# A fused cross-attention and ternary feed-forward kernel: the attention loop regrouped into beats of two key blocks

## The chip, the core and the metric

The kernel runs on one NeuronCore of a Trainium2 chip, as one launch. The core has four compute engines that run side by side, each through its own instruction stream in order: TensorE (PE in the profile, with its weight loads listed apart as PEld), VectorE (DVE), ScalarE (ACT) and GpSimd (POOL). SyncE (SP) only issues transfers here. Matrix products land in PSUM, everything else lives in SBUF; DMA queues move data, and a DMA issued by POOL can add into its target on the way. The metric is device time in microseconds, lower is better; it is given as the median of several runs.

## The reference

Shapes: `x` is 2048 x 256 (the latents), `ctx` is 1601 x 256, four heads of 64, hidden width 1024. Cut to what matters:

```python
lat = layernorm_g_b(layernorm(x));  c = layernorm_g_b(ctx)
q = lat @ W_q;   k, v = split(concat([c, lat]) @ W_kv)      # 1601 + 2048 keys
q, k = rmsnorm(q) / 8, rmsnorm(k)                           # per head of 64
sim = q @ k.T;   sim[:, masked ctx keys] = -big
x = x + (softmax(sim) @ v) @ W_out + b_out                  # 2048 x 256
h = act_quant(layernorm(x)) @ weight_quant(w1).T            # ternary weights, 2048 x 1024
h = silu(depthwise_conv3(h) + conv_b)
x = x + act_quant(h) @ weight_quant(w2).T
```

The softmax needs, for each query and head, the maximum over all keys before the exponentials and the sum of the exponentials after them.

## The kernel before

**Tiling.** The keys are padded to 29 blocks of 128 (`NKB`): blocks 0 to 12 are the context (`NCB` = 13, masked), blocks 13 to 28 are the latents. The queries are cut into four groups of 512, the heads into two pairs, which gives eight *units* `(g, pr)`. A unit works on a tile of keys x (2 heads x 512 queries), 128 x 1024 in float32: scores have the keys on the partitions. The two heads of a pair lie on partition halves, so a score product (`raw_scores`, line 176) is two products that each use 64 rows of the PE array, and a value product (`attend`, line 514) is two products that each fill 64 columns. In the profile the forms are called `64*128` and `128*64`; one float32 product shows as two records, so a block of scores or of values is a group of x4.

**Two passes over the scores.** While unit u is being attended, the scores of unit u+1 are computed once for their maxima (`look_ahead`, line 184, tile `sa`): a context block is copied out of PSUM with its mask added and kept in SBUF (ACT, tile `sg`, 14 buffers in `ring`), a latent block is not kept; DVE reduces either to its maxima (`mxs`). When all 29 blocks are seen, `column_maxima`, `transpose_maxima`, `row_maxima` and `spread_shift` (lines 451 to 495) turn them into the negative maximum per query, as a pair of bfloat16 rows (`rows`) and as a full tile (`nb`). In unit u+1 itself a kept block needs only `sg + nb` (`subtract`, line 498, on DVE) and the exponential on ACT (tile `pt`, five buffers); a latent block is computed again on PE on top of the broadcast shift (`again`, line 502, tile `st`: two bfloat16 products and one float32 score product, shown as x6) and then exponentiated.

**Sums and values.** `attend` adds each `pt` into a sum: context blocks and the last two on POOL (`acc`), the other latent blocks by accumulating DMAs from POOL's queue into `acd` (in the last unit by DVE), and multiplies `pt` with the values into `ot` in PSUM. `finish_unit` (line 540) copies `ot` out on ACT, joins the two sums on POOL, and forms the reciprocal denominators in five further planned pieces: 16 products (`dn`), a reciprocal, eight diagonal matrices on ACT (`dg`), 16 products that spread them (`rd`), a multiply. After every second unit `finish_block` (line 593) runs four times: output projection `po`, residual, layer norm and activation quantization of 128 rows each, the result transposed (`tpq`). In the last unit `weight_tasks` (line 707) quantizes and transposes the feed-forward weights.

**Order.** The loop over steps (lines 745 to 788) takes one key block per step, latent and context blocks in turn, and emits in this order: the exponential two steps on, the look-ahead of one block (sometimes two), the subtraction three steps on or the repeated scores two steps on, then `attend`, then whatever `at(k, ...)` has planned for that step. `InOrder` (line 157) keeps this order on each engine, so all these instructions carry line 165 in the profile, and they are told apart by their tiles. PSUM has three two-bank buffers for scores (`big`, line 148, used by `sa`, `st` and `sh`), one single bank (`bank`) for small results, and one for `ot`. After the loop the feed-forward part runs in `slot(s)` (line 933), with the tail of the plan taken before each slot.

Of the kernel before, what the change touches and what calls it, by code (L numbers as in the profile page):

```python
# [17 lines left out]
P = 128  # L18
# [8 lines left out]
def kernel(  # L27
# [386 lines left out]
    def at(k, *calls):  # L414

        plan.setdefault(k, []).extend(calls)
# [30 lines left out]
    with att:  # L447
# [13 lines left out]
        def transpose_maxima(m4):  # L461
            tp = bank("tpm", [P, P])
            tensor.transpose(tp, m4.rearrange("p a b -> p (a b)"), ident)
            return tp

        def row_maxima(tp):

            nm = sm.tile([P, 32], F32, tag="nm", name="nm", bufs=2)
            vector.tensor_reduce(
                nm, tp.rearrange("p (a i) -> p i a", a=4), AX.X, ALU.max, negate=True  # L470
            )
            hi = sm.tile([P, 32], BF16, tag="hi", name="hi", bufs=2)
            vector.tensor_copy(hi, nm)
            val = sm.tile([P, 32], F32, tag="val", name="val", bufs=2)
# [23 lines left out]
        def subtract(u, j):  # L498

            vector.tensor_tensor(staged[u, j], staged[u, j], shifts[u][1], ALU.add)  # L500
# [13 lines left out]
        def attend(u, j, pt, ot, sums, i):  # L514


            g, pr = units[u]
            acc, acd = sums
            if j < NCB or i >= NKB - 2:
                if j == 0:  # L520
                    gpsimd.tensor_copy(acc, pt)
                else:
                    gpsimd.tensor_tensor(acc, acc, pt, ALU.add)
            elif u == len(units) - 1:
                if i == 0:
                    vector.tensor_copy(acd, pt)
                else:
                    vector.tensor_tensor(acd, acd, pt, ALU.add)
            elif i == 0:
                gpsimd.dma_start(acd, pt)  # L530
            else:
                gpsimd.dma_start(acd, pt, accum_op=ALU.add)
            for hh in range(2):
                h = 2 * pr + hh
                tensor.matmul(
                    ot[halves(hh), :], v_sb[:, j, h * DH : (h + 1) * DH], pt[:, hh, :],
                    start=(i == 0), stop=(i == NKB - 1),
                )

        def finish_unit(k, ot, sums, dst):  # L540

            scalar.copy(dst, ot)
            box = {}
            acc, acd = sums

            def join():
                gpsimd.tensor_tensor(acc, acc, acd, ALU.add)

            def denominators():

                box["dn"] = bank("dn", [P, NSUB, 2])
                for sub in range(NSUB):
                    for hh in range(2):
                        tensor.matmul(
                            box["dn"][:, sub, hh : hh + 1], acc[:, hh, ts(sub, P)], ones[:, 0:1],
                            start=True, stop=True,
                        )

            def inverses():
                box["r"] = sm.tile([P, NSUB, 2], F32, tag="r", name="r", bufs=2)  # L560
                vector.reciprocal(box["r"], box["dn"])

            def diagonals():
                box["dg"] = ptp.tile([P, NSUB, 2, P], F32, tag="pt", name="dg")
                for sub in range(NSUB):
                    for hh in range(2):
                        scalar.activation(
                            box["dg"][:, sub, hh, :], ident, AF.Copy,
                            scale=box["r"][:, sub, hh : hh + 1],
                        )  # L570

            def spread_inverses():
                box["rd"] = bank("rd", [P, NSUB, P])
                for sub in range(NSUB):
                    for hh in range(2):
                        tensor.matmul(
                            box["rd"][halves(hh), sub, :], ones[:, :DH], box["dg"][:, sub, hh, :],
                            start=True, stop=True,
                        )

            def divide():
                vector.tensor_tensor(
                    dst, dst, box["rd"].rearrange("p s q -> p (s q)"), ALU.mult
                )

            for n, call in (
                (1, join), (3, denominators), (4, inverses), (5, diagonals), (6, spread_inverses),
                (7, divide),
            ):
                at(k + n, call)  # L590


        def finish_block(k, qb, oT, sub):
# [47 lines left out]
            for n, call in (  # L641
                (-2, bias), (0, project_out), (1, residual), (2, inverse_deviation), (3, normalize),
                (5, quantize), (6, transpose), (7, spread),
            ):
                at(k + n, call)
# [3 lines left out]
        def quantize_weight(src, i):  # L649
            w_sb, box = [], {}  # L650

            def load():
                for k in range(2):
                    t = ring.tile([P, 2 * QW], F32, tag="sg", name="w_sb")
                    nc.sync.dma_start(t.rearrange("p (a d) -> p a d", d=src.shape[2]), src[:, k])
# [51 lines left out]
        def weight_tasks(k):  # L707
# [5 lines left out]
            for n, call in enumerate(calls):  # L713
                at(k + n, call)
# [5 lines left out]
        order = [NCB + i // 2 if i % 2 == 0 else i // 2 for i in range(2 * NCB)]  # L720
        order += list(range(2 * NCB, NKB))
        early = {i: [i // 2] if i % 2 == 0 else [NCB + i // 2] for i in range(2 * NCB - 1)}
        for n, i in enumerate((6, 12, 18, 24)):
# [271 lines left out]
```

## Time and profile before

| | value |
|---|---|
| median of three runs | 994.49 us (994.21, 994.49, 1006.95) |
| the profiled execution | 1002.59 us, its span 1000.8 us |
| prologue: norms, keys, values, queries, maxima of unit 0 | 0 to about 162 us |
| the eight units: starts of the eight `nb` copies | 162.4, 243.4, 327.8, 422.8, 510.0, 598.3, 681.7, 773.3 us |
| feed-forward part: first `ph` product | 854.7 us, to the end |
| busy over the span: PE, DVE, ACT, POOL | 86%, 80%, 55%, 56% |
| mean granted TensorE clock | 0.906 |

The differences of the `nb` starts are the lengths of units 0 to 6: 81.0, 84.4, 95.0, 87.3, 88.3, 83.4 and 91.6 us, 610.9 us together. Units 2, 4 and 6 also carry the four `finish_block`s of the query group before; they are the longest on average. In the profile a group line gives the line, engine, operation, output from inputs, shapes and count, then busy time and mean duration, then the idle time just before and what ended it. The tile view gives shortest, median and longest duration instead. The chain of waits is the sequence of work, each piece released by the one before, that leads to the last instruction.

### The profile page before, as it was taken

To read this page: it belongs to the slowest core of one execution; us is meant where nothing else is said; L and a number is where in the kernel's file an instruction comes from. 1 tells how busy PE (TensorE), PEld (TensorE's weight loads), DVE (VectorE), ACT (ScalarE), POOL (GpSimd) and SP (SyncE) were. 2 spreads that over 40 slices of the span, in tenths; PEclk is the share of its full clock that TensorE was granted. 3 is DMA by queue.
4 is the path that set the end of the run, shared out by engine and by line. 5 is a ranking of instruction groups with operands and counts; after the bars stand their busy time and mean duration, and the time that the engine had idled before them with its cause. 6 is when DMAs were issued, how large, how long until landed. Compare 5 with 4: busy or idle time off the path is not lost.

```text
span 1000.8 us, 10358 instructions
## 1 busy us (share of the span) xinstructions
PE 859.9 (86%) x3672; PEld 328.0 (33%) x3672; DVE 797.1 (80%) x914; ACT 546.5 (55%) x738; POOL 560.7 (56%) x447
## 2 busy tenths in 40 slices
PE   4788987998999999899989999998998977656564
PEld 3334442322322332233223323223322322434342
DVE  4566456996898689968877987987899897399996
ACT  2456444554555555365555556555553634888792
POOL 2432332655565466555665677556666654777672
PEclk9999998999999899899999999999999977555557
DMA  5000001543455343434543444544434100000000
GB/s 135 22 22 22 1 0 43 105 85 84 84 98 101 77 84 71 77 85 84 105 95 74 85 83 92 100 86 103 84 69 101 63 1 18 4 12 10 13 20 32
DMA packets 29776, 63.28 MB, mean 63 GB/s; under 512 B 7259, under 2 KB 16668, under 8 KB 29724
## 3 DMA queue, kind: packets, MB, share of 16 engines
q0 software_dynamic: 14112, 51.39, 26.2%
q1 hardware_dynamic: 12030, 10.44, 3.4%
q10 hardware_dynamic: 3582, 0.79, 0.4%
q8 instruction: 29, 0.48, 0.2%
q14 instruction: 23, 0.19, 0.1%
HBM read 9.13 MB, written 2.10 MB: 11 GB/s over the span
## 4 chain that ended last, share of the span: by engine, by line
PE 55%; DVE 32%; ACT 5%; issue 4%; DMA 2%; POOL 2%; ACTq 0%; POOLq 0%; DVEq 0%
PE sa L165 16%; PE ot L165 16%; PE st L165 10%; DVE mxs L165 5%; DVE sg L165 5%; PE kv L353 5%; PE sa L179 3%; DVE m L165 2%; DVE y L165 2%; DVE acd L165 2%; DVE t L165 2%; DVE h L165 2%; DVE hi L165 1%; DVE rows L165 1%; DVE qsc L165 1%
## 5 line engine op out<-in xcount | busy, mean ns | idle before, releaser
L165 POOL TENSOR_TENSOR acc<-acc,pt 128x1024 f32<-128x1024 f32 x112 | 282.9, 2526 | 35.3 <-ACT pt L165 34.9
L165 PE MATMUL ot<-pt,v_sb 128*64 128x512 f32 x928 | 252.7, 629 | 2.0 <-ACT pt L165 1.9
L165 DVE TENSOR_TENSOR sg<-sg,nb 128x1024 f32<-128x1024 f32 x104 | 215.7, 2080 | 13.9 <-ACT nb L165 13.9
L165 PE MATMUL sa<-q_un,kT 64*128 64x512 f32 x812 | 223.7, 639 | 2.8 <-DVE mxs L165 2.8
L165 POOL DMA_DIRECT2D acd<-pt x98 | 83.9, 856 | 211.8 <-ACT pt L165 164.0
L165 ACT ACTIVATE sg<-sa,maskc 128x1024 f32<-128x1024 f32 x91 | 101.2, 1112 | 177.2 <-PE sa L165 176.9
L165 ACT ACTIVATE pt<-st 128x1024 f32<-128x1024 f32 x128 | 130.9, 1023 | 76.5 <-PE st L165 76.3
L165 DVE TRANSPOSE_TENSOR_REDUCE mxs<-sa 128x32 f32<-128x1024 f32 x112 | 137.4, 1232 | 35.9 <-PE sa L165 34.9
L165 DVE TRANSPOSE_TENSOR_REDUCE mxs<-sg 128x32 f32<-128x1024 f32 x91 | 112.7, 1238 | 38.5 <-ACT sg L165 38.5
L165 PE MATMUL st<-q_un,kT 64*128 64x512 f32 x512 | 141.1, 630 | 0.0
L165 ACT ACTIVATE pt<-sg 128x1024 f32<-128x1024 f32 x104 | 109.3, 1051 | 41.2 <-DVE sg L165 41.1
L165 PEld LDWEIGHTS sa<-q_un,kT 64*128 64x128 f32 x812 | 63.9, 185 | 137.8 <-issue 90.1
L165 PEld LDWEIGHTS ot<-pt,v_sb 128*64 128x64 f32 x928 | 48.4, 138 | 182.9 <-issue 173.7
L165 PEld LDWEIGHTS st<-q_un,kT 64*128 64x128 f32 x512 | 53.0, 201 | 34.6 <-issue 30.8
L353 PE MATMUL kv<-wkv_sb,feat 128*128 128x512 f32 (+1 forms) x116 | 55.8, 624 | 0.0
L165 PE MATMUL st<-rows,ones 64*128 64x512 bf16 x256 | 52.0, 400 | 1.5 <-DVE mxs L165 1.5
L329 DVE TENSOR_TENSOR nn<-raw,ss 128x512 f32<-128x512 f32 (+1 forms) x23 | 15.7, 681 | 47.0 <-POOL ss L101 47.0
L165 POOL TENSOR_TENSOR pre<-pre,side 128x512 f32<-128x512 f32 x32 | 41.8, 1306 | 14.6 <-DVE pre L165 13.3
L165 ACT ACTIVATE side<-h,cw_sb 128x256 f32<-128x256 f32 x96 | 44.4, 494 | 0.0
L165 PE MATMUL py<-w2T,hq 128*128 128x256 bf16 x128 | 30.4, 418 | 14.6 <-DVE hq L165 14.6
L165 ACT ACTIVATE pre<-h,cb_sb,cw_sb 128x256 f32<-128x256 f32 x64 | 37.4, 584 | 9.8 <-DVE h L165 9.7
L165 ACT ACTIVATE t<-pre 128x512 f32<-128x512 f32 x32 | 36.5, 1141 | 9.4 <-POOL pre L165 9.4
(131 smaller groups left out, 1002.2 us busy)
## 6 DMA issues: line engine op xcount, KB each, us to landing
acd<-pt POOLq DMA_DIRECT2D x98, 512.0 KB, 4.5
tok<-in_x_dram SPq DMA_DIRECT2D x4, 512.0 KB, 3.6
q_un<-in_x_dram SPq DMA_DIRECT2D x4, 512.0 KB, 3.6
w_sb<-in_L_ffn_w_dram SPq DMA_DIRECT2D x4, 512.0 KB, 3.3
out_dram<-res SPq DMA_DIRECT2D x16, 128.0 KB, 1.8
tok<-in_ctx_dram SPq DMA_DIRECT2D x3, 512.0 KB, 4.1
wkv_sb<-in_L_xattn_W_kv_dram ACTq DMA_DIRECT2D x1, 512.0 KB, 8.9
wo_sb<-in_L_xattn_W_out_dram SPq DMA_DIRECT2D x1, 256.0 KB, 8.2
```

The costliest lines, as they stand in the source:

```text
L165: return tc.keep_in_program_order(getattr(self.engine, name)(*args, **kwargs))
L179: tensor.matmul(st[:, hh, :], kT[halves(hh), pr, ts(j, P)], qT[g][halves(hh), pr, :], start=start, stop=True,)
L329: nc.vector.tensor_tensor(nn[:rows, :nb, :].rearrange("p b (h d) -> p b h d", d=DH), raw[:rows, :nb, :].rearrange("p b (h d) -> p b h d", ...
L353: nc.tensor.matmul(kv[:rows, b, :], feat[:, c, c0 + b * rows : c0 + (b + 1) * rows], wkv_sb[:, c, :], start=(c == 0), stop=(c == ND - 1),)
```

## The change

The loop takes *beats* of two blocks instead of steps of one: 13 beats of one latent and one context block, and a 14th of the last three latent blocks. In a beat all scores come first and the two or three value products last. The look-ahead of the next unit is spread over beats 0 to 10 (three blocks a beat, two in beats 2, 5, 7 and 10); the maxima are gathered in beat 11 and the shift is spread in beat 12, with the exponentials always one beat ahead of the values (`following` is the next beat's list of blocks, of unit `v`). POOL does the subtraction, two beats ahead, except for a unit's beats 0 and 1, which DVE does. The sums: first blocks of beats 0 to 12 are accumulated by DMA into `acc`, second blocks by DMA into `acd` in eight beats, and by DVE into a new tile `acv` in beats 0, 3, 6, 9, 12 and 13 (in every beat of the last unit); POOL adds the other two blocks of beat 13 into `acc`. DVE joins the sums, and copies `ot`. The denominators are two products with 512 columns, whose result is inverted by one DVE reciprocal of 128 x 512 in PSUM. Both roundings of the negative maxima are read from PSUM, and `val` lies in PSUM. The weights are loaded through ACT's queue instead of SP's. The planned pieces are placed anew in the middle (before the values) or at the end of a beat.

The diff, cut:

```diff
+    MID, END = 0, 1
+
+    def at(k, call, when):
+
+        plan.setdefault((k, when), []).append(call)
...
         def transpose_maxima(m4):
-            tp = bank("tpm", [P, P])
-            tensor.transpose(tp, m4.rearrange("p a b -> p (a b)"), ident)
+            tp = big("tpm")
+            tensor.transpose(tp[:, 0, :P], m4.rearrange("p a b -> p (a b)"), ident)
             return tp
...
-            vector.tensor_copy(hi, nm)
-            val = sm.tile([P, 32], F32, tag="val", name="val", bufs=2)
+            for dst in (hi, nm):
+                vector.tensor_reduce(
+                    dst, tp[:, 0, :P].rearrange("p (a i) -> p i a", a=4), AX.X, ALU.max,
+                    negate=True,
+                )
+            return tp, nm, hi
+
+        def place_maxima(tp, nm, hi):
+
+            val = tp[:, 1, :32]
             vector.scalar_tensor_tensor(val, hi, second, nm, ALU.mult, ALU.add)
...
+        def subtract(u, j, eng):
+
+            eng.tensor_tensor(staged[u, j], staged[u, j], shifts[u][1], ALU.add)
...
+        def add_up(u, b, n, pt, sums, by_vector):
+            acc, acd, acv = sums
+            if by_vector != (n == 1 and (b % 3 == 0 or b == NB - 1 or u == len(units) - 1)):
+                return
+            if by_vector:
+                if b == 0:
+                    vector.tensor_copy(acv, pt)
+                else:
+                    vector.tensor_tensor(acv, acv, pt, ALU.add)
+            elif b == NB - 1:
+                gpsimd.tensor_tensor(acc, acc, pt, ALU.add)
+            else:
+                dst = acd if n else acc
+                if b == n:
+                    gpsimd.dma_start(dst, pt)
+                else:
+                    gpsimd.dma_start(dst, pt, accum_op=ALU.add)
+
+        def finish_unit(k, ot, sums, dst, only_two):
+
+            vector.tensor_copy(dst, ot)
             box = {}
-            acc, acd = sums
+            acc, acd, acv = sums
 
             def join():
-                gpsimd.tensor_tensor(acc, acc, acd, ALU.add)
+                vector.tensor_tensor(acc, acc, acv, ALU.add)
+                if not only_two:
+                    vector.tensor_tensor(acc, acc, acd, ALU.add)
...
+                box["dn"] = bank("dn", [P, QW])
+                for hh in range(2):
+                    tensor.matmul(
+                        box["dn"][halves(hh), :], ones[:, :DH], acc[:, hh, :],
+                        start=True, stop=True,
+                    )
 
             def divide():
...
+                vector.reciprocal(box["dn"], box["dn"])
+                vector.tensor_tensor(dst, dst, box["dn"], ALU.mult)
+
+            at(k, join, END)
+            at(k + 1, denominators, MID)
+            at(k + 1, divide, END)
...
             for n, call in (
-                (-2, bias), (0, project_out), (1, residual), (2, inverse_deviation), (3, normalize),
-                (5, quantize), (6, transpose), (7, spread),
+                (-1, bias), (0, project_out), (0, residual), (1, inverse_deviation), (2, normalize),
+                (2, quantize), (3, transpose), (3, spread),
             ):
-                at(k + n, call)
+                at(k + n, call, MID if call in (project_out, transpose) else END)
...
+        beats = [[NCB + i, i] for i in range(NCB)] + [list(range(2 * NCB, NKB))]
+        NB = len(beats)
+        AHEAD = NCB - 2
+        early = [[0, 1, 2]]
+        latents = iter(range(NCB, NKB))
+        for i in range(1, AHEAD):
+            early.append([next(latents) for _ in range(1 if i in (2, 5, 7, 10) else 2)] + [i + 2])
...
+        for k in range(len(units) * NB):
...
+                sums = [acp.tile([P, 2, QW], F32, tag="acc", name="acc", bufs=2), None, None]
                 if not ahead:
-                    weight_tasks(k + 8)
...
+                    weight_tasks(k + 4)
+            if b < NB - 2:
+                subtract_all(k + 2, gpsimd)
+            for n, j in enumerate(blocks):
+                add_up(u, b, n, pts[u, j], sums, False)
+            if ahead and b == AHEAD:
                 mx = column_maxima(u + 1)
...
+            looks = [look_ahead(u + 1, j) for j in early[b]] if ahead and b < AHEAD else []
+            for n in range(max(1, len(looks))):
+                for part in looks[n : n + 1]:
+                    list(part)
+                if n == 0:
+                    for j in following:
+                        if j >= NCB:
+                            again(v, j)
+                            pts[v, j] = exponential(v, j)
+                    for j in following:
+                        if j < NCB:
+                            pts[v, j] = exponential(v, j)
+            if ahead and b == AHEAD + 1:
+                spread_shift(u + 1, mx)
+            for call in plan.pop((k, MID), []):
                 call()
...
+            for n, j in enumerate(blocks):
+                attend(u, j, pts[u, j], ot, (b, n) == (0, 0), (b, n) == (NB - 1, len(blocks) - 1))
+            for call in plan.pop((k, END), []):
+                call()
+            if b == 0:
+                sums[1:] = [
+                    acp.tile([P, 2, QW], F32, tag=t, name=t, bufs=1) for t in ("acd", "acv")
+                ]
+            for n, j in enumerate(blocks):
+                add_up(u, b, n, pts[u, j], sums, True)
+                del pts[u, j]
+            if ahead and b == AHEAD:
+                mx = place_maxima(*row_maxima(transpose_maxima(mx)))
+            if b >= NB - 2:
+                subtract_all(k + 2, vector)
+            if b == NB - 1:
+                finish_unit(k + 1, ot, sums, oT[:, pr, :], not ahead)
...
+                        finish_block(k + 5 + 2 * sub, g * NSUB + sub, oT, sub)
```

## The prediction

> **What bounds the kernel now.** I read the page, then the busy shares by stage, then the chain of waits and the timelines inside single units. The attention loop, 162 to 850 us, is where the change works, so the numbers come from there. In a unit without `finish_block`s the chain of waits is pure PE (start, length, what):
>
> ```profile
> 178.33 1.01 PE ot L165 x4
> 179.34 1.06 PE sa L165 x4
> 180.40 1.01 PE ot L165 x4
> 181.41 1.92 PE sa L165 x8
> 183.33 1.07 PE st L165 x6
> ```
>
> Two look-aheads in a row take 1.92 us, one alone 1.06. A second one adds 0.86, so 0.20 is paid on entering from `ot`. `st` right after `sa` pays nothing (1.07 = 0.86 and two bfloat16 products). The PE timeline gives the same for values, two of them 1.94 against 1.08 for one (records overlap by 0.07):
>
> ```profile
> 681.28 0.39 PE L165 MATMUL sh<-rows,ones 64*128 64x512 bf16 x2 [3.21 <-DVE rows L165]
> ...
> 682.68 1.94 PE L165 MATMUL ot<-pt,v_sb 128*64 128x512 f32 x8
> ...
> 686.68 1.08 PE L165 MATMUL ot<-pt,v_sb 128*64 128x512 f32 x4
> ```
>
> A change of form thus costs 0.20 one way and 0.15 back, 0.35 us in every step. The first of these lines shows the second loss: at each unit's end PE waits for the shift (3.21 us here; 22.9 us in seven waits). In some the clock falls too; stages with PE, PEld, DVE, ACT and POOL busy, then granted clock:
>
> ```profile
> 240.00:242.00 2.00, 0.00 (x0) 0.00 (x0) 2.00 (x1) 0.00 (x0) 2.00 (x1) 1.00 0.00 0
> ...
> 244.00:246.00 2.00, 2.00 (x6) 0.29 (x4) 1.54 (x2) 0.82 (x2) 0.00 (x0) 0.52 0.00 0
> ...
> 248.00:250.00 2.00, 2.00 (x12) 0.69 (x10) 0.15 (x1) 1.52 (x3) 2.00 (x2) 1.00 0.66 262
> ```
>
> Some 3 us at half rate lose about 1.5. DVE is close behind PE and bounds the middle of units 2, 4 and 6. Its variable cost is the two-input SBUF work (tile views, shortest/median/longest):
>
> ```profile
> L165 DVE TENSOR_TENSOR sg<-sg,nb x104: 1167/2466/3500, 163.4 to 836.6; 128x1024 f32<-128x1024 f32 x104
> ...
> L165 DVE TRANSPOSE_TENSOR_REDUCE mxs<-sa x112: 1200/1251/1254, 170.0 to 763.3; 128x32 f32<-128x1024 f32 x112
> ...
> L165 DVE CAST hi<-nm x8: 181/1937/2711, 160.3 to 766.8; 128x32 bf16<-128x32 f32 x8
> ...
> L165 DVE TENSOR_REDUCE nm<-tpm x8: 283/292/292, 160.0 to 766.4; 128x32 f32<-128x128 f32 x8
> ...
> L165 DVE RECIPROCAL r<-dn x8: 167/170/197, 263.4 to 864.2; 128x8 f32<-128x8 f32 x8
> ...
> L165 POOL TENSOR_TENSOR acc<-acc,pt x112: 2336/2449/3231, 170.2 to 849.4; 128x1024 f32<-128x1024 f32 x112
> ```
>
> The spread of the first is 2.33 us, one POOL add; operations that read PSUM show none. Last, POOL's timeline where it waits for its own transfers:
>
> ```profile
> 612.69 0.88 POOL L165 DMA_DIRECT2D acd<-pt  x1 [1.76 <-DMA acd<-pt]
> 613.30 2.65 POOL L165 TENSOR_TENSOR acc<-acc,pt 128x1024 f32<-128x1024 f32 x1
> 617.78 0.88 POOL L165 DMA_DIRECT2D acd<-pt  x1 [1.83 <-DMA acd<-pt]
> ```
>
> Adding into one tile by DMA cannot repeat faster than every 5.09 us.
>
> **The change, part by part (per unit).**
>
> *PE order.* Before, 29 steps x 2.07 + 16 `st` x 1.07 = 77.1. After, 29 x (0.86 + 0.86) + 17.1 + 14 x 0.35 = 71.9. Saved: 5.2. A beat with three look-aheads is then 3 x 0.86 + 1.07 + 1.72 + 0.35 = 5.72 us of PE, with two 4.86.
>
> *Denominators.* `dn` took 1.88 and `rd` 0.87 in the chain (257.95 and 268.5 us); two 512-column products of the `ot` form take one value's 0.86. Saved: 1.9. The eight `dg` (0.39 each) leave ACT, which is not bound. The new 128 x 512 reciprocal is not in the trace. The nearest row, 128 x 8 above, takes 170 ns, against 164 for one column (mean of the 16 `qsc` in the groups): about one element per cycle, so 0.17 + 504 x 1.04 ns = 0.70 us. The Trainium skill, "VectorE: DVE Perf Modes" (First, the fixed hardware budget), says that reciprocal divides iteratively with a repeat count of 8. Read as eight cycles per element of that page's 0.96 GHz that is an estimate of 4.3 us, which would stand before the maxima of beat 2. It should make 8 columns 58 ns slower than one; the row shows 6. I take 0.70; the rule would add up to 3.6 us of DVE per unit, of which beat 2, with two look-aheads, absorbs about half: 1.8 x 8 = 14 us more. That end stays in the range.
>
> *The boundary.* Before: 3.3 us of wait and about 1 of slow clock on the mean. After, the maxima are gathered in beat 11 and PE has three `st` and two values before it needs them. Not free: `tpm` now holds one of three `big` buffers until `rows` is read, and the third `st` of beat 12 takes that buffer. PE gets there 2.1 us after `tpm`; DVE needs 0.3 + 0.3 + 0.25 + 0.69 = 1.5 to 3.9 (only `val` still has two SBUF inputs). I take 0.8 of wait. Saved: 3.5.
>
> *Subtractions.* 11 of 13 go to POOL at 2.45 each (27 us), two beats ahead; POOL loses 13 adds (33) and a join, and gets 21 transfers of 0.86 instead of 14. Behind its transfer waits are the subtraction for the next beat but one and, for it, ACT's exponential. That lead covers about one beat; if it is gone, see the third rival.
>
> *DVE.* It loses 27 us of subtractions and gains `acv` (one copy 0.7, five adds), two joins, two subtractions, the `ot` copy (0.6) and the reciprocal. What would an add cost? The Trainium skill, "SBUF — State Buffer" (Who interferes with whom), says that a two-input DVE operation fully blocks while GpSimd reads SBUF, so up to 1.2 + 2.35 = 3.5. The row agrees at its longest, but also shows 1.17. POOL would be reading 2.45 of some 5.7 us, so an unsynchronized hit costs on average 0.43 x 1.2 = 0.5: I take 1.7. By the full lock each is 1.8 dearer; both ends stay in the range.
>
> *New waits.* With three look-aheads the fourth score buffer of a beat waits for the maximum of its first. This closes a loop through DVE: 1.24 maximum + 0.86 scores + 1.11 mask + 1.24 maximum + 0.3 hand-overs = 4.75 us, plus whatever DVE does at the beat's end; beyond 5.72, PE waits. (a) Beat 0: ACT's three masks and two exponentials let the last maximum end about 7.75 us after the beat began; two joins (3.4), a copy (0.7) and the first maximum of beat 1 (1.24) bring it to 13.1, while PE would want the buffer at 5.72 + 3.0 = 8.7. Wait: 4.4, and 0.8 of slow clock behind it. `dn` is behind the same wait on PE. (b) Beat 4 behind the `acv` add of beat 3: 4.75 + 1.7 - 5.72 = 0.7. The adds of beats 6 and 9 run into beats with two look-aheads, whose buffers don't wait for DVE. (c) With `finish_block`s, whose DVE work (1.0 for residual, 2.6 for the rest) is now in clumps at the ends of beats 7, 9 and 11: 1.6 each at beats 8 and 11.
>
> *At nothing.* The plan's other pieces keep their instructions; POOL's bias and deviation (2.4 per block) lie in the 0.8 to 1.7 us per beat that it waits for a transfer. The weight loads move to ACT's queue, four issues in the last unit, where ACT is half idle. Five `pt` buffers: a `pt` is free when its transfer lands, about one beat before it is asked for.
>
> *Transfers.* POOL's own loop: first beats 5.1, pairs 5.3, a second pair 6.1, because `acd` lands some 2.65 us behind `acc` (0.262 of the span in 98 transfers). That is 16.5 per three beats, 66 for twelve, then 5.1 to land, 5.0 for two adds, 2.5 for a subtraction: 78.6 us, a floor for any unit.
>
> **The sum.** Units 1, 3, 5: 5.2 + 1.9 + 3.5 - 5.2 - 0.7 = 4.7 saved, 14. Units 2, 4, 6: the same less 3.2, plus the 1.1 by which DVE held them above PE: 2.6, 8. Unit 0 meets the floor: 81.0 - 78.6 = 2.4. Last unit: the transfer loop alone paces it, 12 x 5.1 + 5.1 + 5.0 + 2.9, begun some 6 us after `nb`: 80 against 81.4, saved 1. Tail: `dg` is on the chain there (2.2 of its 3.1), against a join and the reciprocal: 2 saved. Together 28 of 1002.6: 974.6. The profiled execution is 0.8% above the median; scaled, 967. I say **966 us**.
>
> **The rivals.** *Elastic* (27%): the waits (a) to (c) are absorbed, since DVE's total per unit, some 62 to 76 us, is under PE's. Then every unit falls to the floor of 78.6, with `finish_block`s about 83 (their 5.5 of PE work less what hides): 22 + 26 + 3 saved, 952, scaled 944. For it: DVE's work gets less. Against: three buffers. *Clumps* (18%): the locks are met in full: (a) grows by two joins' 3.6, (b) by 1.8, in the finishing units (c) by 1.8 for the add of beat 9. That is 16 + 22 = 38, so 10 above now: 1004; half way there 986. For it: the row's median is nearer to its longest than to its shortest. Against: in the old order the same `pt` released both POOL's add and DVE's next steps, so the hits were not by chance. *Slower* (10%): the DMA sums pace the loop, and with them POOL's subtractions and ACT's exponentials queued behind. If two queued transfers share the engines so that `acc` lands with `acd`, a beat takes 6.6 us: 12 x 6.6 + 12.6 = 92 per unit, 7 x 4.5 = 32 more, less the 3 of the last part: 1031, scaled 1023. It decides from 6.2 us a beat, where a unit equals the old mean of 87.3. Against it: one queue served in order.
>
> **How the numbers follow.** Likeliest 45%, own range 950 to 985. A change of 2% (974.6 or 1014.4) is about what a measurement tells from none. Faster: 34 of the 45, and the 27: 61%. Same: 11 and 16: 27%. Slower: 10 and 2: 12%. The range, 932 to 1003, leaves out the best of the elastic case and the slow one.
>
> **What would show it.** `sa` and `ot` groups of x8 to x12 with one switch each way; unit lengths near 80 and 88 us; no PE wait for `rows` above 2 us, but waits of some 4 us for `mxs` in beat 1; the reciprocal at 0.7 us; `acc` issues not under 5.1 us apart. It is wrong if the gaps between `acc` issues exceed 6.2, or if PE waits for ACT rather than DVE.

## The result, and the profile after it

| | before | after |
|---|---|---|
| median | 1004.55 us (20 runs, 994.21 to 1007.62) | 996.04 us (20 runs, 990.63 to 1000.14) |
| ratio, 95% interval | | 0.9934 [0.9906, 0.9961] |
| span of the profiled execution | 1000.8 us | 991.0 us |
| units 0 to 6 (differences of the `nb` starts) | 81.0, 84.4, 95.0, 87.3, 88.3, 83.4, 91.6 | 74.7, 81.7, 91.9, 83.2, 91.2, 82.4, 91.0 |
| last `nb` to first `ph` | 81.2 us | 86.4 us |
| first `ph` to the end | 146.3 us | 147.6 us |
| PE busy and idle inside units 0 to 6 | 583.3 and 27.6 us | 546.1 and 50.2 us |

The kernel is 0.7% faster, where 2.9% was forecast. The runs of the kernel before spread from 994 to 1008 us, so the median of twenty lies 10 us above the median of three given ahead of the forecast; ratios are therefore a safer guide than microseconds. The first `ph` product before starts at 854.50 us (the 854.7 above is the second one), and the last two rows go by that. The length of the prologue is no effect of the change: in the profiled runs of kernels that share the changed kernel's prologue it ends between 159.7 and 162.7 us.

PE did get 37 us less to do in the seven units. But it now stands idle for 23 us more there, and the last unit is 5 us longer. The list of what PE waited for in the changed kernel (total us, times, longest) says where the idle time is:

```profile
PE sa L165 <- DVE mxs L165: 36.6, 17, 4.9
PE tpq L165 <- DVE q_un L165: 17.0, 5, 6.6
...
PE ot L165 <- DVE oT L165: 7.0, 4, 3.9
...
PE sh L165 <- DVE rows L165: 1.7, 1, 1.7
```

The last line is the wait that the change was to attack: it was 22.9 us in seven waits, and is 1.7 in one. That one lies in the prologue, where the kernel before had one of 1.72 too, so inside the units the wait is gone altogether. The first line has taken its place: look-aheads that wait until DVE has taken the maxima out of a score buffer. Unit 1 shows one of these waits. First PE's timeline of the changed kernel, from the beginning of beat 1 (start, length, what, and in brackets the idle time before it with its releaser):

```profile
246.79 1.13 PE L165 MATMUL sa<-q_un,kT 64*128 64x512 f32 x4
247.76 0.38 PE L165 MATMUL st<-rows,ones 64*128 64x512 bf16 x2
247.97 1.02 PE L165 MATMUL st<-q_un,kT 64*128 64x512 f32 x4
248.83 1.02 PE L165 MATMUL sa<-q_un,kT 64*128 64x512 f32 x4
253.61 1.13 PE L165 MATMUL sa<-q_un,kT 64*128 64x512 f32 x4 [3.76 <-DVE mxs L165]
254.67 1.71 PE L165 MATMUL dn<-acc,ones 128*64 128x512 f32 x4
256.16 3.01 PE L165 MATMUL ot<-pt,v_sb 128*64 128x512 f32 x8
```

The beat asks for four score buffers before its first value product, and there are three. The fourth request, at 249.85, comes while DVE is still occupied with the end of beat 0. DVE's timeline of the same kernel:

```profile
246.46 2.37 DVE L165 TRANSPOSE_TENSOR_REDUCE mxs<-sg 128x32 f32<-128x1024 f32 x2 [0.43 <-ACT sg L165]
248.75 1.78 DVE L165 TENSOR_TENSOR acc<-acc,acv 128x1024 f32<-128x1024 f32 x1
250.57 1.22 DVE L165 TENSOR_TENSOR acc<-acc,acd 128x1024 f32<-128x1024 f32 x1
251.71 0.68 DVE L165 COPY acv<-pt 128x1024 f32<-128x1024 f32 x1
252.31 2.37 DVE L165 TRANSPOSE_TENSOR_REDUCE mxs<-sa 128x32 f32<-128x1024 f32 x2
...
257.16 3.33 DVE L165 RECIPROCAL dn<-dn 128x512 f32<-128x512 f32 x1
```

The two joins and the copy, 3.6 us, stand right ahead of the two maxima of beat 1, and the first of the two releases PE. What the wait costs does not end with it. The windows by stage of the changed kernel (the number after POOL's is the granted clock):

```profile
252.00:254.00 2.00, 0.39 (x2) 0.30 (x4) 2.00 (x3) 0.00 (x0) 1.63 (x2) 1.00 1.03 193
254.00:256.00 2.00, 2.00 (x8) 0.44 (x6) 0.69 (x2) 1.11 (x1) 2.00 (x2) 0.75 0.71 270
256.00:258.00 2.00, 2.00 (x8) 0.62 (x6) 2.00 (x2) 0.00 (x0) 1.24 (x3) 0.50 0.75 137
258.00:260.00 2.00, 2.00 (x10) 0.51 (x8) 2.00 (x1) 0.00 (x0) 2.00 (x1) 0.90 1.00 184
```

After the wait of 3.76 us the clock is below full rate in the three windows from 254 to 260, for the most part at half: from 254.67 to the next `sa` at 259.09, `dn` and two values take 4.42 us, where at full clock they take 2.73. So this wait costs 3.76 + 1.69 = 5.45 us.

The last unit has another cause. POOL's timeline in it:

```profile
779.46 0.87 POOL L165 DMA_DIRECT2D acc<-pt  x1 [2.34 <-ACT pt L165]
780.07 2.66 POOL L165 TENSOR_TENSOR sg<-sg,nb 128x1024 f32<-128x1024 f32 x1
784.55 0.87 POOL L165 DMA_DIRECT2D acc<-pt  x1 [1.81 <-DMA acc<-pt]
785.15 2.65 POOL L165 TENSOR_TENSOR sg<-sg,nb 128x1024 f32<-128x1024 f32 x1
794.81 0.87 POOL L165 DMA_DIRECT2D acc<-pt  x1 [7.00 <-DMA acc<-pt]
```

The adding transfers of this unit are issued 5.0 to 5.7 us apart (5.09 in the first pair shown), except for one gap of 10.26. At that time the four weight loads of 512 KB, now all issued at once from ACT's queue, were moving; they took 9.3 us in the median to land (3.3 before).

Where numbers of the sum can be read off directly, the tile views of the changed kernel (shortest, median, longest ns) give:

```profile
L165 DVE TENSOR_REDUCE hi<-tpm x8: 291/291/292, 158.3 to 751.8; 128x32 bf16<-128x128 f32 x8
...
L165 DVE TENSOR_TENSOR rows<-tpm,sel x8: 691/691/692, 159.2 to 752.7; 128x512 bf16<-128x512 f32 x8
...
L165 DVE RECIPROCAL dn<-dn x8: 3331/3333/3367, 257.2 to 848.4; 128x512 f32<-128x512 f32 x8
...
L165 DVE TENSOR_TENSOR acv<-acv,pt x48: 1180/1222/4012, 188.8 to 834.5; 128x1024 f32<-128x1024 f32 x48
```

`hi` was spread from 181 to 2711 ns before and is constant now that both its inputs are out of SBUF. The `acv` adds have a mean of 1.85 us, near the 1.7 taken. The reciprocal is 3.33 us, where 0.70 was taken.

### The profile page after: what moved, and what is told of

Its sections match the earlier page's. It is cut to its first block, busy times and chain, and to the rows that moved or that the text cites. A ratio compares the mean times of both kernels' runs of the same rounds, so it can differ in the third digit from the quotient of the medians.

```text
span 991.0 us, 9828 instructions
## 1 busy us (share of the span) xinstructions
PE 809.3 (82%) x3448; PEld 315.8 (32%) x3448; DVE 723.9 (73%) x891; ACT 523.2 (53%) x666; POOL 563.8 (57%) x485
## 5 line engine op out<-in xcount | busy, mean ns | idle before, releaser
L165 PE MATMUL ot<-pt,v_sb 128*64 128x512 f32 x928 | 236.9, 634 | 12.9 <-DVE oT L165 7.0
L165 POOL TENSOR_TENSOR sg<-sg,nb 128x1024 f32<-128x1024 f32 x88 | 235.0, 2671 | 11.7 <-ACT nb L165 11.5
L165 POOL DMA_DIRECT2D acc<-pt x104 | 89.6, 861 | 155.5 <-ACT pt L165 90.7
L165 PE MATMUL st<-q_un,kT 64*128 64x512 f32 x512 | 134.6, 604 | 0.0
L165 PEld LDWEIGHTS sa<-q_un,kT 64*128 64x128 f32 x812 | 69.3, 187 | 174.4 <-DVE mxs L165 72.2
L165 PEld LDWEIGHTS ot<-pt,v_sb 128*64 128x64 f32 x928 | 60.0, 142 | 161.7 <-issue 135.5
L165 DVE TENSOR_TENSOR acv<-acv,pt 128x1024 f32<-128x1024 f32 x48 | 88.7, 1849 | 9.1 <-ACT pt L165 8.6
L165 POOL DMA_DIRECT2D acd<-pt x56 | 52.4, 935 | 45.2 <-DMA acd<-pt 20.7
L165 POOL TENSOR_TENSOR acc<-acc,pt 128x1024 f32<-128x1024 f32 x16 | 46.5, 2905 | 37.4 <-DMA acc<-pt 29.1
L165 DVE TENSOR_TENSOR sg<-sg,nb 128x1024 f32<-128x1024 f32 x16 | 36.6, 2293 | 14.6 <-ACT nb L165 14.6
```

Source lines behind the costliest of these rows:

```text
L165: return tc.keep_in_program_order(getattr(self.engine, name)(*args, **kwargs))
```

## The experiments

Each starts from the changed kernel unless it says otherwise. A ratio is to the kernel before, so the changed kernel's 0.9934 is what it is held against.

**The joins left out** (the denominators of this kernel then come from one of the three sums alone).

```diff
             def join():
-                vector.tensor_tensor(acc, acc, acv, ALU.add)
-                if not only_two:
-                    vector.tensor_tensor(acc, acc, acd, ALU.add)
+                pass
```

> The changed kernel without the two joins on DVE (the denominators then hold only acc). Theory A, the joins at the end of beat 0 are what PE waits for in beat 1: by the trace DVE would reach the first maximum of beat 1 some 3 us earlier, so each wait of 3.0 to 4.9 us falls to about 1, and the slow clock behind it (about 1.5 us) goes too: six times 4 us, 20 to 27 us less than the changed kernel, ratio to the kernel before about 0.97. Theory B, POOL's own loop of transfers (78.6 us a unit) paces the units: less than 5 us.

977.73 us, 0.9777 [0.971, 0.9844], span 973.4. PE in unit 1's beat 1:

```profile
250.82 1.02 PE L165 MATMUL sa<-q_un,kT 64*128 64x512 f32 x4
253.21 1.13 PE L165 MATMUL sa<-q_un,kT 64*128 64x512 f32 x4 [1.36 <-DVE mxs L165]
254.26 1.08 PE L165 MATMUL dn<-acc,ones 128*64 128x512 f32 x4
```

The wait falls from 3.76 to 1.36, and `dn` and the values behind it run at full clock (1.08 and 1.89 against 1.71 and 3.01). The span is 17.6 us shorter, units 0 to 6 alone 19.8 us: theory A, a little short of the 20 to 27 it named, and far from theory B. The joins, 3.0 us in unit 1 and 26.3 us in all, stand on an engine that is busy for only 73% of the span, and yet most of their time shows in the kernel's, because of the place where they stand.

**The reciprocal in slices**, to see what it costs by width.

```diff
-                vector.reciprocal(box["dn"], box["dn"])
+                a = 0
+                for n in (8, 24, 96, 128, 256):
+                    vector.reciprocal(box["dn"][:, a : a + n], box["dn"][:, a : a + n])
+                    a += n
```

> The changed kernel with its one reciprocal of 512 columns cut into five of 8, 24, 96, 128 and 256 columns. Theory A, a fixed part of about 0.1 us that hides small counts and then 6.4 ns for each column (3.33 us for 512): 0.17, 0.23, 0.7, 0.9, 1.7 us. Theory B, one column a cycle as the rows of 1 and 8 columns suggested, and something else about the large one: 0.17, 0.19, 0.27, 0.30, 0.43 us. Time as the changed kernel within 0.5%.

One run, 1000.67 us. The groups of DVE, different shapes apart (busy us, mean ns of one):

```profile
L165 DVE RECIPROCAL dn<-dn 128x256 f32<-128x256 f32 x8 | 14.1, 1766 | 0.3
L165 DVE RECIPROCAL dn<-dn 128x128 f32<-128x128 f32 x8 | 7.7, 966 | 0.3
L165 DVE RECIPROCAL dn<-dn 128x96 f32<-128x96 f32 x8 | 6.1, 766 | 0.3
...
L165 DVE RECIPROCAL dn<-dn 128x24 f32<-128x24 f32 x8 | 2.5, 316 | 0.3
L165 DVE RECIPROCAL dn<-dn 128x8 f32<-128x8 f32 x8 | 1.5, 191 | 2.7 <-PE dn L165 2.7
```

From 24 columns to 256 the slope is (1766 - 316) / 232 = 6.25 ns a column, over about 166 ns that are always paid; 512 columns would be 3.37, and 3.33 was measured. Eight columns take 191 ns, 25 above the fixed part where the slope would add 50, and in the kernel before they took 170, 6 more than one column: so narrow a row could not give the price.

**The reciprocal left out** (this kernel multiplies by the denominator itself).

```diff
-                vector.reciprocal(box["dn"], box["dn"])
                 vector.tensor_tensor(dst, dst, box["dn"], ALU.mult)
```

> The changed kernel without the reciprocal of 512 columns (the values are multiplied by the denominators). Theory A, its 3.33 us stand at the end of beat 1 before a beat with two look-aheads, which absorbs most of it, and count in full only in the tail where DVE is busy throughout: 3 to 8 us less than the changed kernel. Theory B, half of it counts in every unit: 14 us or more.

996.63 us, 0.9912 [0.9875, 0.9949], span 988.1. The interval overlaps the changed kernel's, and its median is not lower; the traces differ by 2.9 us (3.8 without the prologue). So of the 27 us of reciprocals no more than a few show. The likely reason, not tested apart: they stand at the end of beat 1, behind its maxima, and beat 2 has only two look-aheads, so that PE does not wait for a buffer there.

**The weight loads** by SP's queue again, and, in a second kernel, one load per beat over four beats.

```diff
-                    scalar.dma_start(t.rearrange("p (a d) -> p a d", d=src.shape[2]), src[:, k])
+                    nc.sync.dma_start(t.rearrange("p (a d) -> p a d", d=src.shape[2]), src[:, k])
```

```diff
-            calls = [load1, load2, *rest1[:2], ...
+            for n, (load, i) in enumerate(((load1, 0), (load1, 1), (load2, 0), (load2, 1))):
+                at(k - 3 + n, lambda load=load, i=i: load(i), END)
+            calls = [lambda: None, lambda: None, *rest1[:2], ...
```

> The changed kernel with the four weight loads issued from SP's queue at the same beat. Theory A, the loads and the accumulating transfer share the DMA engines, whatever queue issues: POOL's wait of 7.0 us in the last unit stays, time within 2 us of the changed kernel. Theory B, ACT's queue is what makes them slow (9.3 us to landing against 3.3 before): the wait falls to 2 us and about 5 us are saved.

> The changed kernel with the four weight loads spread over beats 1 to 4 of the last unit, one in each, from ACT's queue. Theory A, the pile of four in one beat holds the accumulating transfer back: POOL's longest wait in the last unit falls from 7.0 to about 3 us and 3 to 5 us are saved. Theory B, any load beside the transfer costs its own 1.3 us or more, so nothing is saved.

992.71 us, 0.9915 [0.989, 0.994], and 993.35 us, 0.9929 [0.9892, 0.9966]. From the last `nb` to the first `ph` it is 83.7 and 83.1 us instead of 86.4; POOL's longest wait for its own transfer there is 3.5 and 2.9 instead of 7.0, and the loads land after 5.8 and 3.9 us instead of 9.3. The traces thus give the collision some 3 us; the times, whose intervals overlap, cannot confirm it. So the issuing queue is not the whole cause (spreading the loads on ACT's queue does as much), nor, by this trace, without effect, as theory A of the first run had it.

**The copy of `ot` back on ACT.**

```diff
-            vector.tensor_copy(dst, ot)
+            scalar.copy(dst, ot)
```

> The changed kernel with the copy of ot out of PSUM back on ACT. PE waits for that copy on DVE in four units of the changed trace (0.7, 1.8, 0.7 and 3.9 us), where it stands behind an add and a subtraction. Theory A, it is the queue in front of it: these waits go, and DVE has 0.6 us less before the joins, 5 to 10 us saved. Theory B, the values of beat 0 wait for the exponentials anyway: under 3 us.

998.38 us, 0.9964 [0.9947, 0.9981]: not faster, by the medians 2 us slower. PE's wait for `oT` is gone from the list. But beat 0 now starts sooner, and the fourth request for a buffer with it, while the joins end where they did: PE waits 4.4 to 4.6 us in beat 1 of six units, each time with half clock behind it. A wait was moved in front of another, and theory A fell.

**The order of a beat undone in part:** the first value product of beats 1 to 10 goes back between the scores.

```diff
                             pts[v, j] = exponential(v, j)
+                    if 0 < b and len(looks) > 1:
+                        attend(u, blocks[0], pts[u, blocks[0]], ot, False, False)
...
             for n, j in enumerate(blocks):
+                if n == 0 and 0 < b and len(looks) > 1:
+                    continue
```

> The changed kernel with the first value product of beats 1 to 10 moved between the scores, which undoes the scores-first order there: two changes of form more in each of these beats (0.35 us) and the same work. Theory A, PE's order of work is worth what the sum said: 10 x 7 x 0.35 = 24 us slower than the changed kernel, less what falls into PE's waits, so 15 to 24. Theory B, PE is no longer the bound: under 5 us slower.

985.63 us, 0.9829 [0.9788, 0.987], span 983.3. It was expected slower by theory A, and is 8 to 10 us faster; theory A fell. Unit 1 is not shorter (81.7 us as before): its PE works 2.7 us longer and waits 2.7 us less. The gain lies in units 2, 4 and 6, which are 1.9 to 2.8 us shorter each. PE in unit 1's beat 1:

```profile
247.57 1.02 PE L165 MATMUL st<-q_un,kT 64*128 64x512 f32 x4
248.52 1.08 PE L165 MATMUL ot<-pt,v_sb 128*64 128x512 f32 x4
249.53 1.13 PE L165 MATMUL sa<-q_un,kT 64*128 64x512 f32 x4
253.20 1.13 PE L165 MATMUL sa<-q_un,kT 64*128 64x512 f32 x4 [2.54 <-DVE mxs L165]
```

With the value product in front of it, the fourth request comes 4.27 us into the beat instead of 3.06, the wait is as much shorter, and beats 4, which waited 1.2 us each, do not wait at all. The wait that is left still has slow clock behind it (`dn` takes 1.94 us where 1.08 is full clock). Four score groups in a row had saved changes of form and lost that cover.

**All subtractions on DVE.**

```diff
-                subtract_all(k + 2, gpsimd)
+                subtract_all(k + 2, vector)
```

> The changed kernel with all subtractions on DVE, still two beats ahead: 11 a unit more on DVE at 1.2 to 3.4 us, POOL left with its transfers and two adds. Theory A, PE's waits are on DVE's place in the score-buffer loop (4.75 us and DVE's work at the end of a beat), and each beat now has a subtraction in it: every beat of three look-aheads gets 0.2 to 1.5 us longer, DVE's total rises from some 62 to about 83 us a unit: 20 to 60 us slower than the changed kernel. Theory B, POOL's subtractions come too late for ACT and are themselves the bound: faster.

1008.37 us, 1.0076 [1.005, 1.0102]: 12 to 17 us slower than the changed kernel, less than the least expected. The tile views say why:

```profile
L165 DVE TENSOR_TENSOR sg<-sg,nb x104: 1180/1212/3371, 160.8 to 830.0; 128x1024 f32<-128x1024 f32 x104
...
L165 DVE TENSOR_TENSOR acv<-acv,pt x48: 1181/1208/3400, 188.6 to 850.7; 128x1024 f32<-128x1024 f32 x48
```

With POOL left to transfers and two adds a unit, DVE's median subtraction is 1.21 us; it was 2.47 in the kernel before, where POOL added a block in every second step. Handing the subtraction to POOL is a gain, but less than the old row makes it look.

**No joins, the three sums added in PSUM:** the denominators take each sum as a further accumulated product, half a beat after the unit's end, and `finish_block` starts one beat earlier.

```diff
-            def join():
-                ...
-                for hh in range(2):
-                    tensor.matmul(
-                        box["dn"][halves(hh), :], ones[:, :DH], acc[:, hh, :],
-                        start=True, stop=True,
-                    )
+                parts = [acc, acv] if only_two else [acc, acv, acd]
+                for n, part in enumerate(parts):
+                    for hh in range(2):
+                        tensor.matmul(
+                            box["dn"][halves(hh), :], ones[:, :DH], part[:, hh, :],
+                            start=n == 0, stop=n == len(parts) - 1,
+                        )
...
-            at(k, join, END)
-            at(k + 1, denominators, MID)
+            at(k, denominators, MID)
...
-                        finish_block(k + 5 + 2 * sub, g * NSUB + sub, oT, sub)
+                        finish_block(k + 4 + 2 * sub, g * NSUB + sub, oT, sub)
```

> The changed kernel without joins: the denominators' products take acc, acv and acd one after the other into the same PSUM tile, in the middle of beat 0, and finish_block starts one beat earlier. PE pays two more products of 0.86 us a unit. Theory A (joins on DVE are the wait of beat 1): as without the joins at all, 18 us less than the changed kernel, plus about 10 for PE: 5 to 12 us saved. Theory B, the sums are not ready at beat 0 and PE waits there instead: no gain or slower.

976.02 us, 0.9729 [0.9688, 0.9771], span 971.9: 19 to 20 us better than the changed kernel, more than expected. PE at the beginning of unit 1:

```profile
247.36 1.08 PE L165 MATMUL dn<-acc,ones 128*64 128x512 f32 x4
248.27 1.03 PE L165 MATMUL dn<-acv,ones 128*64 128x512 f32 x4
249.13 1.03 PE L165 MATMUL dn<-acd,ones 128*64 128x512 f32 x4
249.99 1.89 PE L165 MATMUL ot<-pt,v_sb 128*64 128x512 f32 x8
...
253.84 1.88 PE L165 MATMUL sa<-q_un,kT 64*128 64x512 f32 x8
```

Two more products cost 1.72 us of PE. The `sa` x8 of beat 1 runs through, and `oT` has been copied by the time the values need `ot`. Units 1 to 4 are 77.8, 87.0, 77.8 and 86.7 us, 3.9 to 5.4 shorter each; units 5 and 6 gain 0.8 and 2.9. The earlier `finish_block`s were not tried apart, but units 1 and 3 have none, and their 3.9 and 5.4 come from the joins and the place of `dn` alone.

**The `acd` accumulations left out** (those blocks are missing from the denominators).

```diff
-                else:
+                elif n == 0:
                     gpsimd.dma_start(dst, pt, accum_op=ALU.add)
```

> The changed kernel without the accumulating transfers into acd (only the first copy of a unit is left, so seven second blocks a unit are missing in the denominators). POOL issues 14 transfers a unit instead of 21. Theory A, POOL's loop is not what paces the units: under 4 us less than the changed kernel. Theory B, it is (the floor of 78.6 us, with pairs of transfers at 5.3 and 6.1 us a beat): the floor falls to 12 x 5.1 + 12.6 = 73.8, up to 5 us a unit, 15 to 30 us in all.

985.57 us, 0.9823 [0.9772, 0.9873], span 985.3, between the theories. Units 0 to 6: 75.5, 81.9, 89.9, 81.7, 88.6, 80.9, 89.7. The second transfers cost up to 2.6 us a unit, 8 us in units 0 to 6, and do not hold the units at a floor: unit 0 does not get shorter without them. The waits in beat 4 fall from 1.2 or 1.3 us to 0.4; through what the rest was paid was not traced.

**Two chains of transfers in the last unit**, on top of the sums in PSUM: its first blocks go to `acc` and `acd` by turns.

```diff
-                dst = acd if n else acc
-                if b == n:
+                dst = acd if n or (u == len(units) - 1 and b % 2) else acc
+                if b == (dst is acd):
...
-                finish_unit(k + 1, ot, sums, oT[:, pr, :], not ahead)
+                finish_unit(k + 1, ot, sums, oT[:, pr, :], False)
```

> x8_psum_join, and in the last unit the transfers go to acc in even beats and to acd in odd ones, so that each has two beats to land. Theory A, the last unit (about 87 us from nb to the first ph product in the changed kernel) is paced by one chain of transfers at 5.09 us: it gets 8 to 20 us shorter than in x8_psum_join. Theory B, it is DVE or the weights' pieces that pace it: under 4 us.

961.45 us, **0.9578 [0.9541, 0.9615]**, span 959.1: the fastest median found, clear of both kernels. Some of POOL's issues in its last unit:

```profile
776.02 0.87 POOL L165 DMA_DIRECT2D acd<-pt  x1 [3.04 <-DMA acd<-pt]
...
779.60 0.87 POOL L165 DMA_DIRECT2D acc<-pt  x1 [0.32 <-issue]
...
783.01 0.88 POOL L165 DMA_DIRECT2D acd<-pt  x1
```

These three stand 3.4 to 3.6 us apart in place of 5.09. Over the whole unit the thirteen issues take 52.1 us, 4.3 from one to the next, since others wait for ACT's exponentials or, during the weight loads, 3.04 us for their own chain (the first line). The last unit is 77.4 us, against 88.7 with one chain and the same sums.

**Order and loads on top of that:** first both together, then, since the result left open which of them it was, each alone. The edits are those shown above.

> x10_two_chains, with the first value product back between the scores in beats 1 to 10 (as x6_interleave) and the weight loads spread over four beats (as x4_loads_spread). If the gains are of separate waits they add: 5 to 8 us from the order, 3 from the loads, on top of x10_two_chains. If the joins' absence has already removed the waits that the order covers, the order costs: up to 15 us slower than x10_two_chains.

> x10_two_chains plus the weight loads spread over four beats, with the scores still first in every beat. x11_all had both this and the interleaved order, and was 4 us slower than x10_two_chains (965.5 against 961.5). Theory A: the order is what costs there (once the joins are gone, a score buffer is free in time and each change of form is a loss), and the spread loads take some 2 us out of the last unit's transfer chain: 957 to 961 us, about 0.954 of the kernel before, last unit 75 to 77 us. Theory B: the spread loads cost, since their buffers are taken from the kept scores' ring earlier: 964 to 967 us here, with units 1 to 6 unchanged and a longer last unit.

> x10_two_chains plus the first value product of beats 1 to 10 moved back between the scores, the loads as in the changed kernel. Theory A (the order costs once the joins are gone): 964 to 969 us, about 0.963 of the kernel before, with units 0, 1 and 3 some 0.5 to 1 us longer than in x10_two_chains. Theory B (the order is still a gain, as it was with the joins in place, where it brought 8 to 10 us): 953 to 958 us.

Both: 965.51 us, 0.9618 [0.9587, 0.9649]. Loads spread alone: 961.19 us, 0.9585 [0.9536, 0.9635], span 959.2, no change that the times can tell. Its trace shows a gain all the same: POOL's wait of 3.04 us for its own chain is gone, and the last unit is 74.9 us instead of 77.4, hidden in the span by a prologue that ended 2.8 us later.

Interleaved order alone: 968.65 us, 0.9669 [0.9623, 0.9715], span 966.1, so 7 us slower, with units 1 and 3 at 82.9 and 80.7 us against 77.6 and 77.6. The other units do not pay: units 2, 4 and 6 are 0.3 to 1.2 us shorter, 0 and 5 the same. In unit 1 PE is busy for 80.3 us instead of 77.1 and waits 2.2 us for `mxs` in beat 4, with slow clock behind it. The same edit that made the changed kernel 8 to 10 us faster makes this one some 7 slower. What lies between the two in units 1 and 3 is the joins, and with them the earlier `dn`; units 2, 4 and 6 also have their `finish_block`s one beat earlier.

## Why the prediction was right or wrong

The direction was right, and so was the main loss that the forecast named, the wait behind the joins. The size was not: 28 us were summed (the terms as printed give 27.4), and the traces differ by 9.8. Besides, 966 us was scaled to the median of three runs; by the twenty runs the profiled execution of the kernel before was a usual one, which puts the scaled figures about 8 us too low. By ratio 0.971 was forecast and 0.993 measured.

| term of the sum | forecast saved | measured saved |
|---|---|---|
| start, up to the first `nb` | 0 | 1.7 (runs with the same prologue differ by up to 3) |
| unit 0 | 2.4 | 6.3 |
| units 1, 3, 5 | 14 | 7.6 |
| units 2, 4, 6 | 8 | 0.8 |
| last unit | 1 | -5.3 |
| tail | 2 | -1.3 |

**What failed first is the account of units 1 to 6**, 13.6 us short, and in it the new waits. Wait (a) behind the joins was right in its place and nearly in its size (5.2 summed, 5.45 measured in unit 1; 0.8 of it was for slow clock, which took 1.69). The other waits were too small or missing. In unit 1, (b) was 1.23 us for the 0.7 taken. The wait of beat 1's scores is not all: PE also waits 0.66 us for the `ot` copy, which the forecast priced only as DVE time; it is queued behind a subtraction of 3.37 us. And three beats of this unit with three look-aheads (3, 6 and 8) take 5.90 us instead of 5.72, since their last two `sa` groups take 2.06 instead of 1.88. With (a), that is 0.25 + 0.53 + 0.66 + 0.54 = 2.0 us more than forecast, and unit 1 is 2.1 short (2.6 saved for 4.7). That the two agree is in part luck: the 0.8 of wait taken for the boundary did not come, and PE's other work was as much longer. Units 3 and 5 saved 4.0 and 1.0.

In the units with `finish_block`s, (c) was 3.2 us of waits, and 2.95 came: 1.05 for `sa` in beat 9 and 1.90 for `tpq` in beat 11. (DVE's clumps stand at the ends of beats 6, 8 and 10, one beat earlier than the forecast had them.) Missing was the slow clock behind the second. PE in unit 2:

```profile
388.52 1.13 PE L165 MATMUL sa<-q_un,kT 64*128 64x512 f32 x4 [1.04 <-DVE mxs L165]
...
400.74 0.27 PE L165 MATMUL tpq<-ident,yq 128*128 128x128 bf16 x2 [1.90 <-DVE q_un L165]
400.94 2.91 PE L165 MATMUL ot<-pt,v_sb 128*64 128x512 f32 x8
```

The two values take 2.91 us instead of 1.94; the windows from 402 to 406 have a granted clock of 0.50 and 0.71, and 1.7 us are lost, in each of these three units. Units 2, 4 and 6 saved 3.1, -2.9 and 0.6 us. The middle one had least to gain: the seven waits for `rows` before were the one in the prologue and those at the ends of units 0 to 3, 5 and 6, and unit 4 had none.

**"PE order: saved 5.2" was right by itself and wrong as a saving.** The forecast had seen that four requests meet three buffers, and counted the order and the waits as separate terms, net about -0.7 a unit. That was a small loss already in its own numbers, hidden by the other savings. Undoing the order in ten beats gave back 8 to 10 us, so the net loss was about twice as large. With the joins away, the same order is worth 7 us. So the work saved on PE is real: without it, PE is busy 2.7 us longer in unit 1 of the changed kernel, and 2.9 in unit 3 of the form without joins. Whether it becomes time depends on the waits in its place, and the joins in beat 0 (3.0 us of DVE in unit 1, in front of the buffer's release) are the largest of those.

**"At nothing" failed for the weight loads.** Their cover was named as ACT's idle time; what they met was the adding transfer, delayed by some 5 us. The traces of the two other placements give 2.7 to 3.3 us of the last unit's 5.3 back. Against the forecast's own terms the unit is 6.2 us long, 86.4 for 80.2, and the trace shows where. The first issue comes 8.4 us after `nb` and not 6, because POOL's two adds and the subtraction in front of it take 9.8 us instead of 7.5. From the first issue to the last it is 65.5 us instead of 61.2, mostly by the one late transfer. The end takes 12.5 instead of 13.0. That the transfer chain paces this unit held: with two chains it is 11.3 us shorter.

**The tail** lost 1.3 where 2 were to be gained. Leaving out the reciprocal leaves it at 147.5, so that is not the cause; without joins it is 146.3, with the sums in PSUM 145.6. The joins account for about 1.3 to 2.0 of the difference of 3.3; the rest stays open.

**The reciprocal** was taken at 0.70 us, by the nearest row, and is 3.33. The Trainium skill, "VectorE: DVE Perf Modes" (First, the fixed hardware budget), with its iterative divide and repeat count of 8, from which 4.3 was estimated, was much nearer: the slope is 6.25 ns a column, six cycles of the page's 0.96 GHz rather than eight. The forecast set the rule aside because 8 columns cost 6 ns more than one; but at that width the fixed cost hides most of the slope. The 14 us that the rule would have taken off were not lost either: the traces show 3 to 4.

**The floor of 78.6** was wrong: unit 0 took 74.7. It put the transfers of a unit end to end. By the run without `acd`'s accumulations the second ones cost up to 2.6 us a unit and bound nothing at 78.6. That unit 0 saved 6.3 instead of 2.4 is luck: it made up for 3.9 us of the terms that fell short.

**What held:** `rows` waits gone (from the units altogether), constant durations of what reads PSUM, the price of an `acv` add (1.7 taken, 1.85 measured), and the pace of 5.09 us of the adding transfers. **The rivals:** *elastic* fell with the waits. *Clumps*, at half its size, came nearest to the time (986 of 994.5, 0.991, against the measured 0.993) but not by its mechanism: the `acv` adds' median is 1.22 us, so the lock is not met in full. *Slower* fell: no unit grew to its 92 us, and only the last unit is shown to be paced by its transfers.

## What to carry to other kernels

Before grouping products of one form, count how many buffers in a row the group asks for, and what the engine that frees them has in front of it at that moment; the products taken out from between were also cover. Work at a boundary that only adds tiles for a following matrix product can go into that product's PSUM accumulation, where it cost 1.7 us of PE instead of 3.0 us of DVE and a wait. And a price for a wide operation is not to be read from a row a few columns wide, nor a transfer called free without asking which chain of transfers it will run beside.

## What the hardware showed that was not expected

- A DVE reciprocal in PSUM costs 166 ns and 6.25 ns for each float32 column from 24 columns on; 128 x 512 takes 3.33 us.
- Adding transfers of 512 KB into one tile were issued 5.09 us apart. Into two tiles by turns they were 3.4 to 3.6 us apart in the stretch shown, and 4.3 on the mean of the unit. One such transfer beside four loads of 512 KB was late by 5 us.
- After a wait of 3.76 us PE ran below full clock (0.75, then 0.50, then 0.90 in windows of 2 us), which cost 1.7 us. A wait of 2.54 us, in the interleaved order, also had 0.58 and 0.56 behind it; one of 1.36 us, without joins, had none. The length alone does not decide: the waits of 1.90 us for `tpq` in units 2, 4 and 6 of the changed kernel each cost the same 1.7 us, and one of 2.66 in its unit 0 cost nothing (1.00 in the windows behind it).
